# Mixture of experts beside attention: sorting each image's tokens while the next one is attended to

## The chip, the core and the metric

The kernel runs on one core of a Trainium2 chip. The metric is the device time of one execution in microseconds. A core has five engines that each run their own list of instructions in a fixed order and wait for one another through semaphores: TensorE (PE, with its weight loads as PEld), VectorE (DVE), ScalarE (ACT), GpSimd (POOL) and SyncE (SP). Transfers between the device's memory and the core's buffers are issued by SP, ACT or POOL and carried by 16 DMA engines.

## What is computed

Four blocks of a hybrid network work on x of 4 images, 256 channels, 32 x 32 points: 4096 tokens of 256 channels, 1024 to an image. Layer 0 is a Mamba-2 mixer with a squeeze-and-excitation gate, layer 1 a non-local convolution. Layer 3 is an attention of linear kind and an LSTM over 1024 steps. The change is in layer 2:

```python
t = t + _L2_attn_ref(_ln_t(t), Wq, bq, Wk, bk, Wv, bv)      # per image, 1024 x 1024 scores
t = t + _L2_ffn_ref(_ln_t(t), Wg, bg, W1, b1, W2, b2)

# in _L2_ffn_ref, xf = all 4096 tokens, E = 8 experts
gate_logits = xf @ Wg + bg
top_w, top_i = jax.lax.top_k(gate_logits, 2)
top_w = jax.nn.softmax(top_w, axis=-1)
...
h = jax.nn.gelu(xf @ W1[e] + b1[e], approximate=False)
out = out + w_dense[:, e:e + 1] * (h @ W2[e] + b2[e])
```

The normalisation of a token needs only that token, attention needs its image, and which tokens an expert gets needs the gates of all tokens that are counted before.

## The kernel before

x stays in the core's buffers as `s.x`, channels on the partitions, in two halves. The phases run in the order of `PHASES`: `_setup`, `_layer0`, `_layer1`, `_layer2_attention`, `_layer2_experts`, `_layer3` and the LSTM.

`_setup` (L75 to L139) loads x and constants, makes the index tables, and fills `sorted`, a table in the device's memory with 39 x 256 rows of 258 numbers: the normalised token, its weight, and the place where its result goes. Rows that no token takes must be harmless, so 13 transfers of 6 x 128 rows (SP, L137) write zeros and spare places, from two buffers that POOL fills by memset and iota (L132, L133). A pool named `weights` with two buffers holds the weights of a layer (`_weights`, L161).

`_layer2_attention` (L512) multiplies the weights of queries and keys into one matrix `mat` (L528 to L556), normalises all of x over channels (`_layernorm`, L167: PE's averages over the partitions, `mean`, `var`, `wide`), and goes through the images. For an image it makes `q` (L563) and `v` (L576), and then for each of 8 query tiles of 128: scores `p_s` against 1024 keys (L593, 8 matmuls of 512 columns), their maximum (L601 to L603, DVE), exp (L606, ACT), the scale (L610, L611, DVE), 8 transposes (`p_t`, L615), whose copies into `prT` are shared by DVE and ACT (L620, L622). After four query tiles 16 matmuls of 512 columns times the values make the output (L626), which is added to x (L631).

`_layer2_experts` (L763) normalises x again, and `_route` (L634) makes the gates with 64 small matmuls (L649), finds the two best experts of every token, counts by matmul and prefix sum how many tokens each expert has, and gives each expert whole tiles of 256 rows; 2 x 4096 rows fill at most 39 tiles. `_sort` (L737) turns the tokens into rows by transposes and sends 64 scatters of 128 rows (POOL, L757). Then 39 tiles (L784) follow: POOL fetches the weights of the tile's expert (`w`, L786, 128 rows of 16 KB), SP the 256 rows (L793), PE transposes them (`pt`, L801; copy `uT`, L803), 32 matmuls of 256 columns make the hidden layer (`ph`, L808), ACT applies Gelu (L812), 32 more make the output (`po`, L816), DVE scales it (`y`, L821) and POOL scatters it to `results` (L822). Weights, rows and `uT` have three buffers each. A tail (L827 to L852) reads `results` back and adds both shares and the bias to x.

What sets the order: outside of the LSTM, a static scheduler places the instructions of each engine from their dependencies, so an engine's list differs from the order of the code. Pools of buffers are opened and closed; a pool that is opened later may lie on the bytes of a closed one, and its first writer then waits for all users of those bytes.

Of the kernel before, what the change touches and what calls it, by code (L numbers as in the profile page):

```python
# [10 lines left out]
F32 = mybir.dt.float32  # L11
U32 = mybir.dt.uint32
I32 = mybir.dt.int32
# [30 lines left out]
NTILE = 2 * T // TS + E - 1  # L44
ROW = D + 2
# [29 lines left out]
def _setup(s):  # L75
# [50 lines left out]
    s.sorted = nc.dram_tensor("sorted", (NTILE * TS, ROW), F32, kind="Internal").ap()  # L126
    s.results = nc.dram_tensor("results", (2 * T + NTILE * TS, D), F32, kind="Internal").ap()
    n = 6
    with s.tc.tile_pool(name="fill", bufs=2) as pool:
        for i in range(NTILE * TS // P // n):  # L130
            fill = pool.tile([P, n, ROW], F32, name="fill")
            nc.gpsimd.memset(fill[:, :, : D + 1], 0.0)  # L132
            nc.gpsimd.iota(  # L133
                fill[:, :, D + 1 :].rearrange("p a c -> p (a c)"), [[P, n]], base=2 * T + i * n * P,
                channel_multiplier=1, allow_small_or_imprecise_dtypes=True,
            )
            nc.sync.dma_start(  # L137
                s.sorted[bass.ts(i, n * P), :].rearrange("(a p) c -> p a c", p=P), fill
            )  # L139

# [20 lines left out]
def _weights(s, name):  # L161
    w = s.wpool.tile([P, C, NW[name]], F32, name=name, tag="w")
    s.nc.scalar.dma_start(w, s.d[name].rearrange("(k p) n -> p k n", p=P))
    return w
# [37 lines left out]
def _layer0(s):  # L202

    nc, tc = s.nc, s.tc
    w = _weights(s, "w_l0")
    w_zdt, w_xbc = w[:, :, :ZDT], w[:, :, ZDT : ZDT + 512]
    w_out, w_se1 = w[:, :, 772:1028], w[:, :, 1028:1092]
    with ExitStack() as ctx:
# [303 lines left out]
def _layer2_attention(s):  # L512

    nc, tc = s.nc, s.tc
    w = _weights(s, "w_l2")
    s.w_gate = w[:, :, 768:776]
    wq, wk = w[:, :, :D], w[:, :, D : 2 * D]
    scale = D**-0.5
    with ExitStack() as ctx:
        keep = ctx.enter_context(tc.tile_pool(name="l2_keep", bufs=1))  # L520

        mat = keep.tile([P, C, D], F32, name="mat")
        r = keep.tile([P, C], F32, name="r")
        wv = keep.tile([P, C, D + 1], F32, name="wv")
        bv = keep.tile([P, D + 1], F32, name="bv")
        with tc.tile_pool(name="l2_w_ps", bufs=1, space=PSUM) as ps:
            bb = keep.tile([P, C], F32, name="bb")
            nc.vector.tensor_mul(bb, s.col["bq"], s.col["bk"])  # L528
            pm = ps.tile([P, C, D], F32, name="pm")
            pr = ps.tile([P, C], F32, name="pr")  # L530
            pg = ps.tile([P, C], F32, name="pg")
            pb = ps.tile([P, 1], F32, name="pb")
            for m in range(C):
                for k in range(C):
                    nc.tensor.matmul(
                        pm[:, m, :], wq[:, k, bass.ts(m, P)], wk[:, k, :],
                        start=k == 0, stop=k == C - 1,
                    )
                for k in range(C):
                    nc.tensor.matmul(  # L540
                        pr[:, m : m + 1], wk[:, k, bass.ts(m, P)], s.col["bq"][:, k : k + 1],
                        start=k == 0, stop=k == C - 1,
                    )
                for k in range(C):
                    nc.tensor.matmul(
                        pg[:, m : m + 1], wq[:, k, bass.ts(m, P)], s.col["bk"][:, k : k + 1],
                        start=k == 0, stop=k == C - 1,
                    )
            for k in range(C):
                nc.tensor.matmul(pb, s.ones, bb[:, k : k + 1], start=k == 0, stop=k == C - 1)  # L550
            nc.vector.tensor_copy(mat, pm)
            nc.vector.tensor_copy(r, pr)
            nc.vector.tensor_copy(wv[:, :, :D], w[:, :, 2 * D : 3 * D])
            nc.vector.tensor_scalar_mul(wv[:, :, D], pg, scale)
            nc.vector.tensor_copy(bv[:, :D], s.row["bv"])
            nc.vector.tensor_scalar_mul(bv[:, D:], pb, scale)  # L556
# [4 lines left out]
        ps = ctx.enter_context(tc.tile_pool(name="l2_ps", bufs=2, space=PSUM))  # L561
        for b in range(B):
            q = pool.tile([P, C, L], F32, name="q")  # L563
            for m in range(C):
                for i in range(BPI):
                    p = ps.tile([P, W], F32, name="p_mm")
                    for k in range(C):
                        nc.tensor.matmul(
                            p, mat[:, k, bass.ts(m, P)],
                            u[:, k, b * L + i * W : b * L + (i + 1) * W],  # L570
                            start=k == 0, stop=k == C - 1,
                        )
                    nc.scalar.activation(
                        q[:, m, bass.ts(i, W)], p, AF.Identity, bias=r[:, m : m + 1]
                    )
            v = pool.tile([P, TPI, D + 1], F32, name="v")  # L576
            for n in range(TPI):
                p = ps.tile([P, W], F32, name="p_mm")
                for k in range(C):
                    nc.tensor.matmul(  # L580
                        p[:, : D + 1], u[:, k, b * L + n * P : b * L + (n + 1) * P], wv[:, k, :],
                        start=k == 0, stop=k == C - 1,
                    )
                nc.vector.tensor_add(v[:, n, :], p[:, : D + 1], bv)

            for i in range(BPI):
                prT = pool.tile([P, TPI, W], F32, name="prT")
                for j in range(TPB):
# [14 lines left out]
                    nc.vector.tensor_sub(top, c, top)  # L603
                    pr = pool.tile([P, L], F32, name="pr")
# [6 lines left out]
                    nc.vector.tensor_scalar_mul(pr, pr, total)  # L611
                    for g in range(TPI // TPB):
                        p_t = ps.tile([P, TPB, P], F32, name="p_t")
                        for m in range(TPB):
                            nc.tensor.transpose(  # L615
                                p_t[:, m, :], pr[:, bass.ts(g * TPB + m, P)], s.ident
# [6 lines left out]
                for m in range(C):  # L623
                    p = ps.tile([P, W], F32, name="p_mm")
                    for n in range(TPI):
                        nc.tensor.matmul(  # L626
                            p, v[:, n, bass.ts(m, P)], prT[:, n, :],
                            start=n == 0, stop=n == TPI - 1,
                        )
                    xs = s.x[:, m, b, bass.ts(i, W)]  # L630
                    nc.vector.tensor_add(xs, xs, p)  # L631


def _route(s, keep, u):  # L634
# [3 lines left out]
    nc, tc = s.nc, s.tc  # L638
    gate = keep.tile([P, NT, E], F32, name="gate")
    share = keep.tile([P, 2, NT], F32, name="share")  # L640
    slots = keep.tile([P, 2, NT], U32, name="slots")
    wrow = keep.tile([P, NTILE], U32, name="wrow")
    with ExitStack() as ctx:
        pool = ctx.enter_context(tc.tile_pool(name="route", bufs=1))
        ps = ctx.enter_context(tc.tile_pool(name="route_ps", bufs=1, space=PSUM))
        pl = ps.tile([P, NT, E], F32, name="pl")
        for n in range(NT):
            for k in range(C):
                nc.tensor.matmul(  # L649
                    pl[:, n, :], u[:, k, bass.ts(n, P)], s.w_gate[:, k, :],  # L650
                    start=k == 0, stop=k == C - 1,
                )
        lg = pool.tile([P, NT, E], F32, name="lg")
        nc.vector.tensor_add(lg, pl, _bc(s.row["bg"], 1, NT))
        tops, picks = [], []
        for i in range(2):
            top = pool.tile([P, NT], F32, name=f"top{i}")
            nc.vector.tensor_reduce(top, lg, AX.X, ALU.max)
            pick = pool.tile([P, NT, E], F32, name=f"pick{i}")
            nc.vector.tensor_tensor(pick, lg, _bc(top, 2, E), ALU.is_equal)  # L660
            nc.vector.tensor_mul(pick, pick, _bc(s.rank, 1, NT))
            first = pool.tile([P, NT], F32, name=f"first{i}")
            nc.vector.tensor_reduce(first, pick, AX.X, ALU.max)
            nc.vector.tensor_tensor(pick, pick, _bc(first, 2, E), ALU.is_equal)
            if i == 0:
                nc.vector.scalar_tensor_tensor(lg, pick, -3.0e38, lg, ALU.mult, ALU.add)
            tops.append(top)
            picks.append(pick)


        both = pool.tile([P, E, NT], F32, name="both")
        nc.vector.tensor_add(both.rearrange("p e n -> p n e"), picks[0], picks[1])
        flat = both.rearrange("p e n -> p (e n)")
        p_in = ps.tile([P, E, NT], F32, name="p_in")
        nc.tensor.matmul(p_in.rearrange("p e n -> p (e n)"), s.upper, flat, start=True, stop=True)
        p_all = ps.tile([P, E, NT], F32, name="p_all")
        nc.tensor.matmul(p_all.rearrange("p e n -> p (e n)"), s.ones, flat, start=True, stop=True)

        second = share[:, 1, :]
        nc.vector.tensor_sub(second, tops[1], tops[0])  # L680
        nc.scalar.activation(second, second, AF.Exp)
        first = share[:, 0, :]
# [608 lines left out]
```

## Time and profile before

| what | us |
|---|---|
| median of 3 runs (3884.6 to 3886.61) | 3886.4 |
| profiled execution | 3885.56 |
| its span, first to last instruction | 3883.9 |
| layer 0, first `px` (L232) at | 63.2 |
| layer 2's attention, four images | 561.9 to 893.6 |
| second LayerNorm, gates, routing, scatters, first weights | 893.6 to 1081.85 |
| 39 tiles of the experts | 1081.85 to 1676.06 |
| tail, to layer 3's LayerNorm | 1736 |
| LSTM, to the end | 1940 to 3884 |

The profile is taken of one execution. Its page tells for each engine the busy time, cuts the span in 40 slices of 97.1 us with the busy share in tenths, and lists the transfers. A window is a stretch of the span, with each engine's busy time and number of instructions in it, the mean clock granted to TensorE, the share of the DMA engines' time and the GB/s. A line of a group reads: source line, engine, operation, result<-operands, shape, count | busy time and mean ns of one | idle time of the engine just before, and what ended it. PE is busy for 3461.2 of 3883.9 us (89%), DVE 52%, ACT 31%, POOL 9%; the mean granted clock is 0.945.

### The profile page before, as it was taken

The page shows a single profiled execution, that of the slowest core. Times are in us where ns is not written, and L with a number is a line of the kernel's source. Part 1 is how long each engine was busy: PE and PEld are TensorE (multiplying, and loading weights), DVE is VectorE, ACT ScalarE, POOL GpSimd, SP SyncE. Part 2 cuts the span into 40 slices and gives each one's busy share as a digit, 9 for nine tenths or more (in the row PEclk, how much of TensorE's full clock was granted, in tenths as well). Part 3 has the DMA queues.
Part 4 walks back from the last instruction along what each step waited for, and adds up shares of the span by engine and source line. Part 5 has one row for each costly group of instructions (what it writes and reads, how often), then busy time and mean ns, then how long its engine had stood idle before and what let it go on. Part 6 is the DMA issues. An engine that isn't in the chain of part 4 may idle for free.

```text
span 3883.9 us, 147409 instructions
## 1 busy us (share of the span) xinstructions
PE 3461.2 (89%) x65882; PEld 2641.0 (68%) x65882; DVE 2008.8 (52%) x7905; ACT 1220.7 (31%) x4983; POOL 331.4 (9%) x404
## 2 busy tenths in 40 slices
PE   8557769998289999999899999999999999999988
PEld 3344324444178888864588888888888888888776
DVE  3587354342301111113367677777777776777666
ACT  2233212121122222213233343434434334343333
POOL 2055000000611111100000000000000000000000
PEclk8778979997599999998899999999999999999999
DMA  4000000000254554420000000000000000000000
GB/s 173 0 1 1 8 0 0 0 1 0 94 207 167 172 180 165 164 93 0 10 4 5 10 4 5 10 5 10 4 4 10 4 10 4 5 9 5 9 4 9
DMA packets 54619, 152.20 MB, mean 39 GB/s; under 512 B 5464, under 2 KB 42016, under 8 KB 48992
## 3 DMA queue, kind: packets, MB, share of 16 engines
q0 software_dynamic: 12432, 100.64, 7.4%
q1 hardware_dynamic: 39616, 37.39, 3.1%
q8 instruction: 515, 8.44, 0.9%
q10 hardware_dynamic: 1936, 4.75, 0.4%
q14 instruction: 120, 0.98, 0.1%
HBM read 109.58 MB, written 33.18 MB: 37 GB/s over the span
## 4 chain that ended last, share of the span: by engine, by line
PE 71%; DVE 17%; ACT 5%; issue 3%; DMA 2%; POOL 0%; ACTq 0%; DVEq 0%; POOLq 0%; SPq 0%
PE p_c L1142 10%; PE ph L808 7%; PE po L816 7%; DVE turned L1171 6%; PE p_c L1133 6%; PE p_i L1133 4%; PE p_o L1133 4%; PE p_o L1142 4%; PE p_i L1142 4%; PE beside L1086 4%; PE p_mm L626 3%; ACT a_o L1172 2%; DVE hs L1187 2%; DMA sorted<-row,slots 2%; PE p_s L593 2%
## 5 line engine op out<-in xcount | busy, mean ns | idle before, releaser
L1172 ACT ACTIVATE add<-turned 128x8 f32<-128x8 f32 x1024 | 214.4, 209 | 1027.4 <-DVE turned L1171 1027.4
L1142 PE MATMUL p_c<-w_v,hs 128*4 128x64 f32 x16368 | 415.9, 219 | 71.1 <-DVE hs L1187 68.8
L1133 PE MATMUL p_c<-xg,shift 128*128 128x64 f32 x2048 | 445.7, 299 | 0.0
L1142 PE MATMUL p_o<-w_v,hs 128*4 128x64 f32 x16368 | 416.3, 219 | 0.0
L1142 PE MATMUL p_i<-w_v,hs 128*4 128x64 f32 x16368 | 416.0, 219 | 0.0
L1133 PE MATMUL p_i<-xg,shift 128*128 128x64 f32 x2048 | 407.8, 281 | 0.0
L1133 PE MATMUL p_o<-xg,shift 128*128 128x64 f32 x2048 | 396.0, 275 | 0.0
L1171 DVE STREAM_TRANSPOSE turned<-p_c 128x64 f32<-128x64 f32 x1024 | 255.3, 249 | 262.4 <-PE p_c L1142 227.9
L1133 PEld LDWEIGHTS p_c<-xg,shift 128*128 128x128 f32 x2048 | 304.7, 188 | 117.6 <-issue 0.3
L1142 PEld LDWEIGHTS p_c<-w_v,hs 128*4 128x4 f32 x16368 | 227.2, 85 | 193.4 <-DVE hs L1187 120.1
L1133 PEld LDWEIGHTS p_o<-xg,shift 128*128 128x128 f32 x2048 | 310.9, 192 | 0.3
L808 PE MATMUL ph<-uT,w 128*128 128x256 f32 x1248 | 281.2, 384 | 32.6 <-DVE uT L803 28.2
L1133 PEld LDWEIGHTS p_i<-xg,shift 128*128 128x128 f32 x2048 | 304.6, 188 | 0.4 <-issue 0.3
L1187 DVE TENSOR_TENSOR hs<-a_o,th 128x8 f32<-128x8 f32 x1024 | 171.1, 167 | 244.2 <-ACT th L1185 244.2
L812 ACT ACTIVATE hT<-ph,w 128x256 f32<-128x256 f32 x312 | 147.6, 473 | 436.8 <-PE ph L808 436.8
L808 PEld LDWEIGHTS ph<-uT,w 128*128 128x128 f32 x1248 | 235.3, 191 | 72.3 <-DVE uT L803 36.8
L1142 PEld LDWEIGHTS p_o<-w_v,hs 128*4 128x4 f32 x16368 | 281.0, 87 | 0.1
L1142 PEld LDWEIGHTS p_i<-w_v,hs 128*4 128x4 f32 x16368 | 280.9, 87 | 0.1
L816 PE MATMUL po<-w,hT 128*128 128x256 f32 x1248 | 275.7, 379 | 0.0
L1171 DVE STREAM_TRANSPOSE turned<-p_i 128x64 f32<-128x64 f32 x1024 | 272.2, 266 | 0.1
L816 PEld LDWEIGHTS po<-w,hT 128*128 128x128 f32 x1248 | 237.1, 190 | 32.2
L1171 DVE STREAM_TRANSPOSE turned<-p_o 128x64 f32<-128x64 f32 x1024 | 255.4, 249 | 0.2 <-PE p_o L1142 0.2
(312 smaller groups left out, 4572.5 us busy)
## 6 DMA issues: line engine op xcount, KB each, us to landing
sorted<-fill SPq DMA_DIRECT2D x13, 774.0 KB, 4.4
row<-sorted SPq DMA_DIRECT2D x39, 258.0 KB, 2.7
y_in<-results SPq DMA_DIRECT2D x16, 512.0 KB, 4.9
x<-in_x_dram SPq DMA_DIRECT2D x8, 512.0 KB, 9.9
out_dram<-x SPq DMA_DIRECT2D x64, 64.0 KB, 1.7
results<-y,place POOLq DMA_INDIRECT x78, 2.6
w_l<-in_w_l_dram ACTq DMA_DIRECT2D x1, 1092.0 KB
sorted<-row,slots POOLq DMA_INDIRECT x64, 2.5
```

Of the source, the lines that this page charges most:

```text
L593: nc.tensor.matmul(p_s[:, h, :], q[:, k, q0 : q0 + P], u[:, k, b * L + h * W : b * L + (h + 1) * W], start=k == 0, stop=k == C - 1,)
L626: nc.tensor.matmul(p, v[:, n, bass.ts(m, P)], prT[:, n, :], start=n == 0, stop=n == TPI - 1,)
L808: nc.tensor.matmul(ph, w1[:, k, bass.ts(m, P)], uT[:, k, :], start=k == 0, stop=k == C - 1,)
L812: nc.scalar.activation(hT[:, m, :], ph, AF.Gelu, bias=b1[:, m : m + 1])
L816: nc.tensor.matmul(po, hT[:, m, bass.ts(a, P)], w2[:, m, :], start=m == 0, stop=m == NHC - 1,)
L1086: nc.tensor.matmul(p[bass.ts(i, R), :], rows[:, k, bass.ts(g, R)], w_u[:, k, at : at + GQ // GC], start=k == 0, stop=k == C - 1, tile_posi ...
L1133: nc.tensor.matmul(p[:, :H], shift[:, row * B : row * B + P], xg[n][:, g, bass.ts(i, H)], start=True, stop=t == 0,)
L1142: nc.tensor.matmul(p[R * i : R * i + B, :H], hs[:, t - 1, bass.ts(k, B)], w_v[:, k, i * GQ + g * H : i * GQ + (g + 1) * H], start=False, s ...
L1171: nc.vector.transpose(zt.rearrange("p c w -> p (c w)"), pz[g][:, :H])
L1172: nc.scalar.activation(dst.rearrange("p (c b) -> p c b", c=C), zt[:, :, :B], f)
L1187: nc.vector.tensor_mul(h, a_o, th)
```

## The change

`sorted` gets a fixed region of 4096 rows for every expert, and 128 rows behind them for spare rows. It is filled by 32 transfers of 8 x 128 rows from one tile of zeros. With fixed regions a token's row depends only on the tokens ahead of it, so images can be sorted one after another.

`_layer2_weights` now runs second, before layer 0, and leaves `mat`, `wv` and the gates' weights minus their mean in constant buffers. Layers 0, 2 and 3 have weight pools of their own.

`_head` does for one image what LayerNorm, `_route` and `_sort` did for all: it turns x into rows, takes mean and variance by token with bn_stats, rstd by Newton steps on DVE, gates by 8 matmuls in quarters of the array, choice, counts, slots, and 8 row tiles with 16 scatters. It is a generator that yields 89 times; `_layer2_attention` runs parts of the head of image b−1 between the steps of image b's query tiles. `_first_tiles` makes a table of 16 full tiles from the counts of the first three images; these tiles run first, and the last image's head and the table of the other 23 (`_other_tiles`) are parts between their steps. The rows of a tile are fetched by two indirect transfers from POOL. The dependency between the gathers of the 16 full tiles and the last image's scatters, which touch other rows, is left out.

The diff, cut to what the steps need:

```diff
-    s.sorted = nc.dram_tensor("sorted", (NTILE * TS, ROW), F32, kind="Internal").ap()
+    s.sorted = nc.dram_tensor("sorted", (E * T + P, ROW), F32, kind="Internal").ap()
     s.results = nc.dram_tensor("results", (2 * T + NTILE * TS, D), F32, kind="Internal").ap()
-    n = 6
-    with s.tc.tile_pool(name="fill", bufs=2) as pool:
-        for i in range(NTILE * TS // P // n):
-            fill = pool.tile([P, n, ROW], F32, name="fill")
-            nc.gpsimd.memset(fill[:, :, : D + 1], 0.0)
-            nc.gpsimd.iota(
-                fill[:, :, D + 1 :].rearrange("p a c -> p (a c)"), [[P, n]], base=2 * T + i * n * P,
-                channel_multiplier=1, allow_small_or_imprecise_dtypes=True,
-            )
+    n = 8
+    with s.tc.tile_pool(name="fill", bufs=1) as pool:
+        fill = pool.tile([P, n, ROW], F32, name="fill")
+        nc.gpsimd.memset(fill, 0.0)
+        for i in range(E * T // P // n):
             nc.sync.dma_start(
                 s.sorted[bass.ts(i, n * P), :].rearrange("(a p) c -> p a c", p=P), fill
             )
+        last = pool.tile([P, ROW], F32, name="last")
+        nc.vector.memset(last[:, : D + 1], 0.0)
+        nc.vector.tensor_scalar_add(last[:, D + 1 :], s.token[:, :1], float(2 * T))
+        nc.sync.dma_start(s.sorted[E * T :, :], last)
...
-    w = _weights(s, "w_l0")
+    ctx0 = ExitStack()
+    w = _weights(s, ctx0.enter_context(tc.tile_pool(name="l0_w", bufs=1)), "w_l0")
...
+def _layer2_weights(s):
...
+        pool = ctx.enter_context(tc.tile_pool(name="l2_w", bufs=1))
+        ps = ctx.enter_context(tc.tile_pool(name="l2_w_ps", bufs=1, space=PSUM))
+        w = _weights(s, pool, "w_l2")
+        wq, wk, w_gate = w[:, :, :D], w[:, :, D : 2 * D], w[:, :, 768:]
...
+            nc.tensor.matmul(pg, s.avg, w_gate[:, k, :], start=k == 0, stop=k == C - 1)
+        nc.vector.tensor_copy(s.mat, pm)
+        nc.vector.tensor_copy(s.r, pr)
+        nc.vector.tensor_copy(s.wv[:, :, :D], w[:, :, 2 * D : 3 * D])
+        nc.vector.tensor_scalar_mul(s.wv[:, :, D], pc, scale)
+        nc.vector.tensor_copy(s.bv[:, :D], s.row["bv"])
+        nc.vector.tensor_scalar_mul(s.bv[:, D:], pb, scale)
+        nc.vector.memset(s.wg, 0.0)
+        nc.vector.tensor_sub(s.wg[:, :, :E], w_gate, _bc(pg, 1, C))
...
+def _layer2(s):
...
+            one=ctx.enter_context(tc.tile_pool(name="moe_one", bufs=1)),
+            pool=ctx.enter_context(tc.tile_pool(name="moe_head", bufs=2)),
+            w=ctx.enter_context(tc.tile_pool(name="moe_w1", bufs=1)),
+            row=ctx.enter_context(tc.tile_pool(name="moe_row", bufs=3)),
+            scatters=[], full=[],
...
+        first = _layer2_attention(s, m)
+        _layer2_experts(s, m, first)
...
+            parts = _head(s, m, b - 1, psum) if b > 0 else iter(())
+            def beside(n):
+                for _ in range(n):
+                    next(parts, None)
...
                     nc.vector.tensor_sub(top, c, top)
+                    beside(4)
                     pr = pool.tile([P, L], F32, name="pr")
...
                     nc.vector.tensor_scalar_mul(pr, pr, total)
+                    beside(4)
                     for g in range(TPI // TPB):
...
+                    beside(3)
...
+            for _ in parts:
+                pass
+            if b == B - 1:
+                first = _first_tiles(s, m)
+    return first
...
+def _head(s, m, b, psum):
+    nc = s.nc
+    n0 = b * TPI
+    x = m.one.tile([P, TPI, D], F32, name="x_rows")
+    mv = m.pool.tile([P, TPI, 2], F32, name="mv")
+    for n in range(TPI):
+        p = psum()
+        for k in range(C):
+            nc.tensor.transpose(p[:, bass.ts(k, P)], s.xt[:, k, bass.ts(n0 + n, P)], s.ident)
+        yield
+        stats = m.pool.tile([P, nc.vector.BN_STATS_DIM], F32, name="stats")
+        nc.vector.bn_stats(stats, p[:, :D])
+        nc.scalar.copy(x[:, n, :], p[:, :D])
+        yield
+        nc.vector.bn_aggr(mv[:, n, :], stats)
+        yield
...
+    p = psum()
+    for k in range(C):
+        for i in range(Q):
+            nc.tensor.matmul(
+                p[bass.ts(i, R), : L // Q], s.wg[:, k, :],
+                s.xt[:, k, b * L + i * (L // Q) : b * L + (i + 1) * (L // Q)],
+                start=k == 0, stop=k == C - 1, tile_position=(0, R * i),
+            )
+    yield
+    raw = m.pool.tile([P, L // Q], F32, name="raw")
+    nc.scalar.copy(raw, p[:, : L // Q])
...
+    upto = m.pool.tile([P, E, TPI], F32, name="upto")
+    upto_flat = upto.rearrange("p e n -> p (e n)")
+    nc.vector.tensor_tensor_scan(
+        upto_flat, m.go_on.rearrange("p e n -> p (e n)"), p_all, 0.0, ALU.mult, ALU.add
+    )
...
+        nc.vector.tensor_add(m.counts, before, upto[:, :, TPI - 1])
+        nc.vector.tensor_add(at, before, m.first)
...
+    for n in range(TPI):
+        row = m.pool.tile([P, 2, ROW], F32, name="row")
+        nc.vector.tensor_scalar(
+            row[:, 0, :D], x[:, n, :], mv[:, n, :1], rstd[:, n : n + 1], ALU.subtract, ALU.mult
+        )
+        nc.scalar.activation(
+            row[:, 1, :D], x[:, n, :], AF.Identity,
+            bias=shift[:, n : n + 1], scale=rstd[:, n : n + 1],
+        )
+        nc.gpsimd.tensor_copy(row[:, :, D:], pair[:, n])
+        yield
+        for i in range(2):
+            done = nc.gpsimd.indirect_dma_start(
+                m.views[2 * (n0 + n) + i], bass.IndirectOffsetOnAxis(slots[:, i, n : n + 1], 0),
+                row[:, i, :], None,
+            )
+            if b == B - 1:
+                m.scatters.append(done)
+        yield
...
+def _first_tiles(s, m):
...
+    nc.vector.tensor_scalar(edges, m.marks[:, :NCH], float(TS), float(TS), ALU.mult, ALU.add)
+    nc.vector.tensor_tensor(over, _bc(m.counts, 2, NCH), _bc(edges, 1, E), ALU.is_ge)
+    full = m.one.tile([P, E], F32, name="f_full")
+    nc.vector.tensor_reduce(full, over, AX.X, ALU.add)
+    expert, mine, first = _table(s, m, "f", NFULL, full)
...
+    rows = _weight_rows(s, m, "f", expert)
...
+def _other_tiles(s, m, taken):
...
+        wp = body.enter_context(tc.tile_pool(name="moe_w", bufs=2))
+        hp = body.enter_context(tc.tile_pool(name="moe_h", bufs=2))
...
+        def last_image():
+            yield from _head(s, m, B - 1, psum)
+            yield from _other_tiles(s, m, taken)
+        parts = last_image()
+        for j in range(NTILE):
+            if j == NFULL:
+                for _ in parts:
+                    pass
+                rows, slots, added = m.others
+            i = j if j < NFULL else j - NFULL
+            w = (wp if j % 3 else m.w).tile([P, NEXP], F32, name="w")
+            nc.gpsimd.indirect_dma_start(
+                w, None, s.d["w12"], bass.IndirectOffsetOnAxis(rows[:, i : i + 1], 0)
+            )
+            w1 = w[:, : C * HID].rearrange("p (k n) -> p k n", k=C)
+            w2 = w[:, C * HID : C * HID + NHC * D].rearrange("p (k n) -> p k n", k=NHC)
+            b1 = w[:, C * HID + NHC * D :]
+            row = m.row.tile([P, A, ROW], F32, name="row")
+            for a in range(A):
+                got = nc.gpsimd.indirect_dma_start(
+                    row[:, a, :], None, s.sorted,
+                    bass.IndirectOffsetOnAxis(slots[:, i, a : a + 1], 0),
+                )
+                if j < NFULL:
+                    m.full.append(got)
...
+                nc.scalar.activation(hT[:, n, :], ph, AF.Gelu, bias=b1[:, n : n + 1])
+                if n % 2:
+                    next(parts, None)
+                    next(parts, None)
...
+        for got in m.full:
+            for put in m.scatters:
+                for one, other in ((got, put), (put, got)):
+                    tc.declare_no_dep(
+                        one.ins, other.ins, reason="the last image's rows follow those of full tiles"
+                    )
...
+        s.wpool = ctx.enter_context(s.tc.tile_pool(name="l3_w", bufs=1))
...
-    w = _weights(s, "w_l3")
+    w = _weights(s, s.wpool, "w_l3")
...
-    _setup, _layer0, _layer1, _layer2_attention, _layer2_experts, _layer3,
+    _setup, _layer2_weights, _layer0, _layer1, _layer2, _layer3,
...
-    s.wpool = ctx.enter_context(tc.tile_pool(name="weights", bufs=2))
```

## The prediction

> **What bounds the kernel now.** I read the slices of the page first, to see where PE stops, then windows over these stretches, the chain of waits across them, the fill tile, and one image of attention by line. The whole kernel is a chain through PE, with two holes:
>
> ```profile
> PE   8557769998289999999899999999999999999988
> ...
> PEclk8778979997599999998899999999999999999999
> DMA  4000000000254554420000000000000000000000
> ```
>
> A slice is 97.1 us. In slices 9 to 11 PE falls and its clock goes to half: that is the LayerNorm, gates and sorting between attention and experts. In slice 0 the DMA engines work: loads and the fill of `sorted`. The windows (PE busy first, the last three columns are clock, DMA share, GB/s) and the chain give the sizes:
>
> ```profile
> 26.00:30.00 4.00, 4.00 (x10) 1.46 (x9) 1.22 (x1) 0.33 (x1) 1.97 (x3) 1.00 1.00 341
> 26.00:56.00 30.00, 23.39 (x38) 6.50 (x37) 13.12 (x10) 5.13 (x5) 14.04 (x20) 0.75 0.79 269
> ...
> 893.60:943.00 49.40, 42.72 (x81) 12.32 (x80) 23.31 (x18) 10.42 (x10) 0.18 (x1) 0.85 0.00 0
> 943.30:971.00 27.70, 27.48 (x128) 27.38 (x128) 0.49 (x4) 0.00 (x0) 0.00 (x0) 0.50 0.00 1
> 971.00:983.00 12.00, 2.05 (x4) 1.18 (x4) 10.11 (x31) 1.51 (x2) 0.00 (x0) 0.50 0.21 66
> 983.00:1067.00 84.00, 20.30 (x64) 9.66 (x64) 22.15 (x136) 11.93 (x32) 60.67 (x63) 0.50 0.28 98
> ```
> ```profile
> 1067.05 2.49 DMA sorted<-row,slots
> 1071.46 10.35 DMA w<-in_w_dram,wrow
> 1081.85 8.83 PE ph L808 x32
> ```
>
> Attention's last matmul ends at 893.6. Then come 49.4 us of LayerNorm, 27.5 of gates, 12 of DVE routing, 84 of scatters (POOL sends 64, one per 1.3 us) and 15 until the first expert weights are there: 188.2 us to the first `ph` at 1081.85. This is what the change attacks. The fill costs nothing today: layer 0 starts beside it, and only one thing waits for its end:
>
> ```profile
> who waited for it (us, times):
>   POOL fill L132: 32.7, 11
>   POOL xbc L213: 4.7, 1
> ```
>
> That second line is the warning. `xbc` has no data from the fill; it waits because its pool lies on bytes that the fill pool gave back.
>
> **Basis.** The profiled execution took 3885.56 us (span 3883.9, 1.66 around it), 0.84 under the median of 3886.4.
>
> **1. The start: +119.** The new `sorted` has 32,896 rows of 1032 bytes, 33.95 MB instead of 10.3. Layer 2's weight pool is now opened second and lies on the closed fill pool. In the instruction order of the changed kernel, ACT's load of `w_l2` waits for the last fill on all the fill's semaphores. PE's order opens with the matmuls on these weights, so the first LayerNorm's `mean`, which stands behind them, waits too, and `w_l0` lies on `w_l2`'s bytes. So nothing of layer 0 starts before the fill ends. Its rate is not on view with 32 transfers in a row. The windows with the DMA engines full (share 1.00) show 341 GB/s, those from 20 to 23 us 332; I take 336. With only two tiles in turn it was 269 at a share of 0.79. The weights and images around 14 to 20 us reached 397. So: loads before the fill end at 14.4 (3.2 + 4.5 MB at about 400); 33.95 MB at 336 is 101 us, 115.7; its end 1.3 later, 117; `w_l2` 4.4 (as the 768 KB load of `w_l3`) 121.4; the weight product 3.6 warm in before (477.13 to 480.7), about 6 at half clock with its copies 6.4: 127.8. LayerNorm as layer 1's, 49.8: 177.6; up to `px` 4.3: 181.9. In before `px` L232 began at 63.2. Difference +119. By 397 GB/s the fill is 85 us, +102; by 269 it is 127, +145.
>
> The Trainium skill, page "DMA: Bandwidth & Descriptors", section "Specifications", gives about 358 GB/s as one core's limit towards HBM. An estimate by that page is 95 us of fill and some 6 us less in the sum; the window with 397 GB/s here is above that figure.
>
> **2. The weight product leaves layer 2: −1.** The copies stood at 508.96 to 510.5, right after layer 1; matmuls were hidden there already.
>
> **3. Images 1 to 3 with a head beside them: +33.** An image takes 82.1 us now, with PE at 77.5 (8 x 3.44 `p_s`, 8 x 1.05 transposes, 6.87 `q`, 7.1 `v`, 27.5 `av`). The rows of one image:
>
> ```profile
> L593 PE MATMUL p_s<-u,q 128*128 128x512 f32 x64 | 28.9, 594 | 0.9 <-ACT pr L606 0.9
> ...
> L601 DVE TENSOR_REDUCE top<-p_s 128x1 f32<-128x1024 f32 x8 | 9.8, 1224 | 7.4 <-PE p_s L593 7.4
> ...
> L615 PE MATMUL p_t<-ident,pr 128*128 128x128 f32 x64 | 8.8, 282 | 3.6 <-DVE pr L611 3.6
> ...
> L611 DVE TENSOR_SCALAR pr<-pr,total 128x1024 f32<-128x1024 f32 x8 | 6.0, 751 | 0.2
> ```
>
> From `p_s` to the transposes the chain is 1.22 + 0.21 + 0.16 on DVE, 1.11 + 0.19 exp, 0.16 + 0.75 on DVE = 3.8 us; the next `p_s` covers 3.44. So PE already waits about half a microsecond per query tile, and what DVE puts into that chain comes on top. A head brings PE 16 transposes (2.1), 8 gate matmuls of 256 columns (at `po`'s 6.92 / 32 = 0.216 each, 1.7), 2 transposes and 2 counts (0.6): 4.4. It brings DVE some 17 us: 8 bn_stats and 8 row writes at 0.42 (as the sort's copies of 256 elements, L749), about 55 small ones at 0.16 to 0.21 (as L602 and L603); DVE has 31 of 82 busy, so it has room. It brings POOL 16 scatters of 0.96. Floor per image 4.4, with all else in gaps. Upper end 18: of the 8 parts put between the steps of each query tile's chain, seven at 0.25 stand in it, 1.7 x 8 = 13.6, plus 4.4. What decides for the middle is the row ring: two row buffers, each free only when its scatters have landed (0.96 + 2.5), and ACT's and DVE's row writes wait for that with the next `prT` copies queued behind them. Following the order by hand I get 3.6 in an image's first half and about 8 in its second (some 5 of it that wait): 12, 12 and 9. Range 13 to 55.
>
> **4. From attention to the first `ph`: −176.6.** Where 188.2 us stood there are now the last scatters of image 2, a small table on DVE, and tile 0's gathers. POOL has tile 0's weight load ahead of the last scatters, and what POOL sends after a weight load lands with it: results scatter after `w` at 1126.0 landed at 1137.2. Then six gathers of 1 us, 2.5 landing, transposes and the copy `uT`: 11.6 us. Bounds 4 (nothing queued) and 15: −184 to −173.
>
> **5. The tiles: +15.8.** 39 tiles at 15.30 (7.17 `ph`, 6.92 `po`, 1.2 gap) now have the last image's head within tiles 0 to 4: PE 4.4; `uT` of tile 4 behind row writes that wait for scatters, about 7; about 1 in tile 3; a first tile at a cold clock +2; against the 594.2 measured +1.4 from rounding to the steady period. ACT changes between Exp and Gelu (1.28 a table load), covered by three `ph` buffers; without them +2.6. Range 8 to 25. The later tiles keep their period: gathers take 78 x 0.96 = 75 us more of POOL, which has 109 of 594 busy, and `row` is asked for three tiles ahead.
>
> **6. Tail, layer 3, LSTM: 0.** Their weights now load after the tail, 4.4 us, beside LayerNorm's 50.
>
> **Sum:** 119 − 1 + 33 − 176.6 + 15.8 = −9.8, so 3875.8 on the profiled execution's basis, about 3876. What a measurement can tell from no change is 0.2%, 7.8 us. So the gain of the sort is nearly eaten by the larger fill.
>
> **Rivals.**
> - *The fill is faster, or the heads fit into gaps* (+102, or +15 for the heads): 3859 or 3858, both 3841; about 3855. For it: 397 GB/s exists in the trace. Against: that was with rows of 3 to 4 KB, and PE's waits.
> - *The fill does not hold the start* (its pool's bytes not waited for, so the change does not do what I read): 3757. Only `xbc`'s wait and the order speak, both against it.
> - *Slower: the fill at the rate of two in flight,* 269 GB/s. 127 us, place: the first 145 us, 3902. It decides from 286 GB/s downwards (118.6 us); at 306 the two kernels are equal. For it: the long window of 30 us. Against: that one had to wait for POOL's memsets, the new one does not. A fill paced like the single transfers (774 KB in 4.4 us, 176 GB/s) would take 193 us: 3968.
> - *Slower: DVE or the row ring becomes the bound of a query tile,* 20 a head rather than 11: 3903.
> - *Slower: the period of the tiles grows,* because `row` comes from POOL behind `w`: 1 us each, 3915. The Trainium skill, same page, section "Issuing engine by pattern", speaks against this move: simple loads belong to Sync, whose path is called generally faster. It has no price there; the rows show 2.7 us for SP's `row` and 2.5 for POOL's scatters.
>
> **How the numbers follow.** Forecast (3866 to 3886): 0.38, of it 0.20 faster and 0.18 same. Fast fill or cheap heads 0.22; fill not waited for 0.03; slow fill 0.14; DVE or ring 0.13; period 0.07; far above 0.03. From the slower cases 0.04 end within 0.2%. Faster 0.45, same 0.22, slower 0.33. Range 3844 to 3910: outside lie the fill not waited for, the lower end of cheap (0.06), most of period (0.05), far above and the tops of the slow ones (0.03), 0.20 together.
>
> **What would show it.** The last `sorted<-fill` landing near 117 and `px` near 182; images 1 to 3 at 91 to 94 us with waits of ACT's rows on scatters; about 12 us between the last `p_mm` and the first `ph`; tiles at 15.3 after the fourth or fifth. I am wrong if PE is busy in layer 0 before the fill has landed, if the images stay at 86 or pass 100, or if tiles 20 to 38 take 16.

## The result and the profile after

The changed kernel takes 3894.8 us (median of 12 runs, 3892.0 to 3900.8) against 3885.6 for the kernel before (12 runs): ratio 1.0024, with a 95% interval of 1.0015 to 1.0033. The forecast was 9.8 us less; it became 9.2 more. The profiled execution has a span of 3893.4 us, 9.5 above that of before. Stage by stage, from the two traces:

| stage | before | after | difference | forecast |
|---|---|---|---|---|
| to attention's first matmul | 561.9 | 699.35 | +137.4 | +118 |
| four images | 331.7 | 364.4 | +32.7 | +33 |
| attention's end to first `ph` | 188.2 | 12.1 | −176.2 | −176.6 |
| 39 tiles | 594.2 | 610.1 | +15.9 | +15.8 |
| tail, layer 3, LSTM | 2207.8 | 2207.5 | −0.3 | 0 |
| sum | | | +9.5 | −9.8 |

Four rows of five are as forecast; the first one alone turns the sign. The slices of the changed kernel's page show both sides of the trade:

```profile
PE   0592866989889999999899999999999999999988
...
PEclk9995988899999999998999999999999999999999
DMA  9400000000155444530000000000000000000000
```

The hole that was in slices 9 to 11 is gone, and a new one stands in slice 0 and the first third of slice 1, where PE does nothing while the DMA engines fill `sorted`. The windows of the changed kernel (PE busy first; the last columns are clock, DMA share and GB/s) are: the fill, image 0 without a head, image 1 with one, the gap, the tiles.

```profile
40.00:100.00 60.00, 0.00 (x0) 0.00 (x0) 0.00 (x0) 0.00 (x0) 0.00 (x0) 1.00 1.09 295
...
699.35:784.05 84.70, 80.19 (x240) 41.38 (x241) 30.02 (x59) 18.15 (x29) 0.00 (x0) 0.96 0.00 0
784.05:878.30 94.25, 84.20 (x279) 43.85 (x278) 43.00 (x135) 24.11 (x46) 17.31 (x24) 0.93 0.07 23
1063.70:1075.80 12.10, 2.24 (x10) 1.56 (x9) 1.90 (x6) 0.00 (x0) 7.67 (x8) 0.68 0.38 98
1075.80:1685.90 610.10, 574.16 (x2682) 495.56 (x2682) 87.50 (x253) 159.19 (x333) 197.76 (x209) 0.99 0.47 167
```

In the first of them no engine works at all: 295 GB/s, with the DMA engines full. The answer on the tile `last`, whose transfer is the fill's end, names who stood behind it:

```profile
who waited for it (us, times):
  POOL xbc L219: 128.4, 1
  DVE bb L537: 123.6, 1
```

`bb` is the first operation of `_layer2_weights`, a product of two columns of constants that is written to the new weight pool (PE's first matmul follows it at 132.6), and `xbc` belongs to layer 0. Neither reads a byte of the fill. The chain of waits at the jump from attention to the experts:

```profile
1048.95 8.31 DMA sorted<-row,slots
...
1061.29 0.98 POOL sorted L872
...
1062.58 2.93 DMA sorted<-row,slots
...
1065.77 0.99 POOL row L1052
...
1072.11 2.73 DMA row<-sorted,f_slots
...
1075.03 0.70 DVE uT L1069
...
1075.78 5.49 PE ph L1074 x12
```

The last scatters of image 2, a landing, row gathers of about 1 us each, a landing, the copy, and the first `ph`: the sequence that was forecast, 12.1 us for 11.6. The first line is a scatter that POOL sent behind tile 0's weight load (at 1045.49): it landed after 8.31 us, where the median of all 64 scatters is 2.8.

### The profile page after: what moved, and what is told of

The parts are those of the page before. It is cut to its first block, busy times and chain, and to the rows that moved or that the text cites. A ratio compares the mean times of both kernels' runs of the same rounds, so it can differ in the third digit from the quotient of the medians.

```text
span 3893.4 us, 147430 instructions
## 1 busy us (share of the span) xinstructions
PE 3397.3 (87%) x65762; PEld 2606.6 (67%) x65762; DVE 2016.6 (52%) x8082; ACT 1228.0 (32%) x5013; POOL 399.5 (10%) x490
## 4 chain that ended last, share of the span: by engine, by line
PE 70%; DVE 16%; ACT 5%; SPq 3%; issue 3%; DMA 2%; POOL 1%; ACTq 0%; DVEq 0%; POOLq 0%
PE p_c L1417 10%; PE ph L1074 7%; PE po L1085 7%; DVE turned L1446 7%; PE p_c L1408 6%; PE p_i L1408 4%; PE p_o L1408 4%; PE p_o L1417 4%; PE p_i L1417 4%; PE beside L1361 4%; SPq L138 3%; PE p_mm L695 3%; PE p_s L659 2%; ACT a_o L1447 2%; DVE hs L1462 2%
```

## The experiments

A run is compared with runs beside it, since the same kernel differs by some us from group to group: the kernel before took 3893.8 us (7 runs) beside the first four runs (long rows, bytes kept, large fill, three in flight) and 3883.6 us (15 runs) beside the others, on another chip. The changed kernel was run again only beside the others, so the first four are read by the moments in their traces as well. A time with no number of runs is that of one execution, without an interval.

### Long rows in the fill

```diff
-                s.sorted[bass.ts(i, n * P), :].rearrange("(a p) c -> p a c", p=P), fill
+                s.sorted[bass.ts(i, n * P), :].rearrange("(p a) c -> p a c", p=P), fill
```

> The changed kernel, with one edit: each of the 32 fills writes, from a partition, 8 rows that lie side by side (8256 bytes in one piece) instead of 8 rows that lie 128 rows apart (1032 bytes each). Same bytes, same zeros. Theory A (the fill is paced by its small pieces): the fill goes from 295 GB/s to about the 420 GB/s that loads with long rows show in the changed kernel's windows at 8 to 14 us, so from about 115 us to 81, and all that stands behind it comes earlier: the last fill lands near 98 instead of 132 and the time is about 3861. Theory B (writes to the device's memory are the limit, whatever their pieces): 295 GB/s again, about 3895.

Measured: 3862.5 us, 31.3 below the kernel before beside it, and in the window of the fill:

```profile
20.00:80.00 60.00, 0.00 (x0) 0.00 (x0) 0.00 (x0) 0.00 (x0) 0.00 (x0) 1.00 1.01 422
```

The fill's last transfer landed at 96.4 instead of 132.1, and the first `px` moved by the same, from 202.0 to 166.3. Theory A: the same bytes, from the same tile, to the same rows, are paced by the length of the pieces.

### The fill's bytes kept

```diff
-    n = 8
-    with s.tc.tile_pool(name="fill", bufs=1) as pool:
+    n = 4
+    for pool in (s.const,):
```

> The changed kernel, with the tile of zeros and the tile of spare rows taken from the constant pool (and 64 fills of 4 rows a partition, as there is room for no more), so that no later pool lies on their bytes. Theory A (the start is held only because layer 2's and layer 0's weight pools, and xbc, lie on the bytes of the closed fill pool): the fill runs beside layer 0, the first px comes near 75 instead of 202, and the time is about 3768. Theory B (the weight loads stand behind the fill on the DMA engines, or layer 0 suffers from a fill beside it): px not before 120, time above 3810.

Measured: 3774.0 us (4 runs), 0.969 of the kernel before (0.9674 to 0.9706). The rows of the first `px` matmuls, in the changed kernel and in this run, and this run's window of the fill:

```profile
L238 PE MATMUL px<-u,w_l x128: 592/592/1219, 202.0 to 284.3; 128*128 128x512 f32 x128
...
L238 PEld LDWEIGHTS px<-u,w_l x128: 190/190/338, 77.1 to 158.5; 128*128 128x128 f32 x128
...
20.00:140.00 120.00, 109.09 (x264) 48.77 (x265) 39.35 (x52) 28.02 (x45) 0.00 (x0) 0.89 1.07 261
```

The first `px` came at 77.1. The fill ran from 13 to about 155, at 261 GB/s between 20 and 140 (294 in the changed kernel, with fills of twice the size and nothing beside them), and layer 0 did not suffer from it: from `px` to attention's first matmul are 496.4 us here and 497.4 in the changed kernel. Theory A: the 125 us by which `px` moved are the price of a pool's address, not of the fill.

### The large fill in the kernel before

```diff
+        extra = nc.dram_tensor("extra", (22 * 8 * P, ROW), F32, kind="Internal").ap()
+        more = pool.tile([P, 8, ROW], F32, name="more", bufs=1)
+        nc.gpsimd.memset(more, 0.0)
+        for i in range(22):
+            nc.sync.dma_start(
+                extra[bass.ts(i, 8 * P), :].rearrange("(a p) c -> p a c", p=P), more
+            )
```

> The kernel before, with 22 more transfers of 8 x 128 rows of zeros to a table of their own after its 13 fills, from a tile of the same fill pool: 33.6 MB written in all, nothing else changed. Theory A (the wait is for the bytes of the fill pool): xbc waits for the last of them, about 56 + 23.3 MB at 295 GB/s = 135 us, layer 0's first px or its copy comes some 75 us later than in the kernel before, time about 3960. Theory B (a larger fill alone, beside layer 0, costs nothing): 3886.

Measured: 3963.9 us, 70.1 above the kernel before. The answer on the tile `more`'s table:

```profile
who waited for it (us, times):
  DVE xbc L245: 77.3, 1
  POOL xbc L220: 66.8, 1
```

Theory A. The line that was harmless before (`xbc`, 4.7 us) is the whole price as soon as the fill is long. Here layer 0's LayerNorm still ran beside the fill, its weights lying elsewhere, so the price is 70 and not 125.

### Three fills in flight, and two

```diff
+        fills = [pool.tile([P, n, ROW], F32, name=f"fill{k}") for k in range(3)]
+        for fill in fills:
+            nc.gpsimd.memset(fill, 0.0)
         for i in range(E * T // P // n):
+            fill = fills[i % 3]
+            if i > 2:
+                nc.gpsimd.memset(fill[:, :1, :1], 0.0)
```

> The changed kernel, with three tiles of zeros in turn and a memset of one column ahead of each reuse, so that no more than three fills are in flight, where the changed kernel has about four (each lands 15.2 us after it was issued, one every 3.5 us). Theory A (the rate falls with the number in flight; in the kernel before, the bursts with two in flight showed 345 to 350 GB/s): about 330 GB/s, 103 us, time about 3882. Theory B (the sustained rate is what it is): 295 GB/s or less, 3895 or more.

Measured: 3903.1 us, 9.2 above the kernel before beside it, as the changed kernel was in the first measurement, and 286 GB/s from 20 to 120. Theory B. The same with two tiles:

> As the run with three in flight, with two tiles of zeros in turn: two fills in flight, as in the kernel before, but with a memset of one column between them instead of 1.5 us of POOL. Theory A (two in flight of these short rows run at 340 to 350 GB/s, three or more at 290): windows at 340 GB/s while both run, some gaps, on the whole about 310 GB/s, fill 110 us, about 5 us less than the changed kernel. Theory B (the bursts of the kernel before were fast because each followed a pause, and the sustained rate is 290): windows at 290 and gaps on top, on the whole 270 GB/s or less, 126 us, some 10 us more than the changed kernel.

Measured: 3901.6 us, 4.7 above the changed kernel's median beside it. The window of the fill:

```profile
20.00:120.00 100.00, 0.00 (x0) 0.00 (x0) 0.00 (x0) 0.00 (x0) 2.55 (x26) 1.00 1.02 285
```

Neither theory has the number: 285, where A said about 310 and B 270 or less. The 4.7 us are not the fill's: `px` began at 204.2 here and at 204.3 in the changed kernel beside it, attention even 1.4 us earlier, and the whole difference between the two profiles lies behind the experts' tiles. Cut into pieces of a quarter of a microsecond, the stretch from 45 to 55 us goes between 78 and 376 GB/s. So bursts of 340 to 355 do exist with these rows, and slack follows. The number in flight isn't what sets the mean: with two, three and four it is 285, 286 and 294. Why the bursts end is not settled.

### Pairs of rows

```diff
-                s.sorted[bass.ts(i, n * P), :].rearrange("(a p) c -> p a c", p=P), fill
+                s.sorted[bass.ts(i, n * P), :].rearrange("(b p a) c -> p b a c", p=P, a=2),
+                fill.rearrange("p (b a) c -> p b a c", a=2)
```

> The changed kernel, with two rows side by side in each piece of a fill (2064 bytes instead of 1032; 8256 gave 422 GB/s, 4128 gave 406 beside layer 0). Theory A (each piece costs a fixed time on its DMA engine beside its bytes: from 1032 bytes at 295 and 8256 at 422 GB/s, with 16 engines, 56.0 and 313 ns a piece, so 35.6 ns a kilobyte and 19 fixed): 2064 bytes take 93 ns, 356 GB/s, a fill of 95 us, about 20 us less than the changed kernel. Theory B (short of some length the rate is that of the short rows): 295 GB/s, no change. Theory C (over 2 kB the rate is full): 415 GB/s, 33 us less.

Measured: 3867.9 us, 29.0 below the changed kernel beside it, and steady:

```profile
20.00:80.00 60.00, 0.00 (x0) 0.00 (x0) 0.00 (x0) 0.00 (x0) 0.00 (x0) 1.00 1.06 379
```

Between A (356) and C (415); theory B fell. By 16 engines, a piece of 1032, 2064 and 8256 bytes took 56, 87 and 313 ns (16 x bytes / rate). A line through the two longer ones has about 12 ns a piece beside the bytes; the 1032-byte piece lies 7 ns above it. So a fixed time a piece, which is an estimate from these rates, explains most, not all, of the slow fill.

### The changed kernel again

> The changed kernel unedited, so that the runs beside it can be compared with it on the same chip. It should stand to the kernel before as measured, 1.0024.

Measured: 3896.9 us (6 runs), ratio 1.0032 (1.0019 to 1.0044): the small loss stands in a second set of runs.

### Eight row buffers for a head

```diff
-        row = m.pool.tile([P, 2, ROW], F32, name="row")
+        row = m.pool.tile([P, 2, ROW], F32, name="row", bufs=8)
```

> The changed kernel with eight buffers instead of two for the row tiles of a head, one for each of its 8 row tiles; nothing else. Theory A (half of what a head costs is ACT's and DVE's row writes waiting for scatters, with the attention's own copies and maxima queued behind them): the three images with a head lose about 5 us each, the wait ahead of the ph of the fifth tile goes (8.35 us in the changed kernel), time about 22 less than the changed kernel's. Theory B (a head costs what its instructions take on PE and DVE, wherever they wait): within 5 us of the changed kernel.

Measured: 3874.5 us (10 runs), 22.4 below the changed kernel beside it, ratio to the kernel before 0.9976 (0.9966 to 0.9985). The waits of the changed kernel between 784 and 1064 us (who <- for whom: total, times, longest) show what went; the three lines on `sorted` are absent in this run's answer, and PE's is 12.6:

```profile
ACT row L865 <- DMA sorted<-row,slots: 38.0, 17, 8.9
...
DVE row L862 <- DMA sorted<-row,slots: 34.4, 16, 8.0
...
PE p_t L683 <- DVE pr L678: 27.8, 5, 9.2
...
POOL row L869 <- DMA sorted<-row,slots: 5.5, 2, 4.9
```

Against the changed kernel beside it, the images with a head became shorter by 6.5, 4.3 and 3.4 us, and the jump from attention to the first `ph` by 6.4, from 12.2 to 5.8. Theory A has the sum; one part of it fell. The wait in the tiles did not go, the tiles became shorter by 1.4 us only. It moved from the fifth tile to the sixth, and the timeline (start, duration, engine, line; in brackets the idle time before) names the cause:

```profile
1129.37 0.98 POOL L1044 DMA_INDIRECT w<-in_w_dram,f_rows  x1 [0.30 <-DMA sorted<-row,slots]
...
1131.94 0.98 POOL L1052 DMA_INDIRECT row<-sorted,f_slots  x1 [0.31 <-issue]
1133.23 0.97 POOL L1052 DMA_INDIRECT row<-sorted,f_slots  x1 [0.30 <-issue]
...
1139.44 0.17 DVE L1061 CAST place<-row 128x2 uint32<-128x2 f32 x1 [19.86 <-DMA row<-sorted,f_slots]
...
1141.04 2.50 PE L1074 MATMUL ph<-uT,w 128*128 128x256 f32 x5 [6.88 <-DVE uT L1069]
```

POOL sent the head's scatters first, then the weights of a later tile, then this tile's rows, which landed behind the weights: 6.1 us after the second was sent, 2.73 in the chain above. In the changed kernel it is the fifth tile that waits: its `uT` stands behind a row write on DVE (at 1148.4) that waited for a scatter.

### All of it together

```diff
-    with s.tc.tile_pool(name="fill", bufs=1) as pool:
+    s.fill = ExitStack()
+    for pool in (s.fill.enter_context(s.tc.tile_pool(name="fill", bufs=1)),):
...
+    s.fill.close()
     nc, tc = s.nc, s.tc
     with ExitStack() as ctx:
         m = SimpleNamespace(
...
-    _setup, _layer2_weights, _layer0, _layer1, _layer2, _layer3,
+    _setup, _layer0, _layer2_weights, _layer1, _layer2, _layer3,
```

with long rows (here 4 side by side, 4128 bytes a piece, in 64 fills) and the eight row buffers as above.

> Three edits together: the fill pool stays open until layer 2 (64 fills of 4 rows a partition), the fills write rows that lie side by side, layer 2's weight product stands behind layer 0, and eight row buffers for a head. If the start was held by the bytes alone: px near 63 as in the kernel before, so 139 less than the changed kernel, and 22 less from the ring: 161 less than the changed kernel, about 3735 by the first measurement. If the ring is nothing: about 3757. If the fill beside layer 0 costs DMA time that layer 0 needs: more than 3770.

Measured: 3737.1 us (4 runs), ratio to the kernel before 0.9625 (0.9609 to 0.9641), 159.8 below the changed kernel. `px` begins at 61.8, attention at 560.0 (561.9 before), and the fill runs beside layer 0 at

```profile
20.00:80.00 60.00, 49.36 (x99) 18.05 (x99) 26.66 (x23) 11.82 (x15) 0.00 (x0) 0.80 1.03 405
```

with 49 of 60 us of PE busy in the same window, where the changed kernel had none.

## Why the prediction was wrong

**Step 1, the start: the step that failed.** The mechanism was right: nothing of layer 0 before the fill's end, with `bb`, PE's weight product, `mean` and `w_l0` in a row behind it. The size was not: +118 forecast at attention's start (119 less 1), +137.4 measured. Of these 19.4 us:

- 15.1 are the fill, a term that was mis-sized. The step put it so: "The windows with the DMA engines full (share 1.00) show 341 GB/s, those from 20 to 23 us 332; I take 336." The last fill landed at 132.1 and not at 117. The rate over 100 us was 294 GB/s; the same bytes in pieces of 2064 and 8256 bytes went at 379 and 422, so the length of the piece set it. The windows of 3 and 4 us were bursts of a transfer that paused every few us. The 30 us window at 269 was put aside because its fills waited for POOL's memsets; with that wait cut to a memset of 0.1 us, and nothing beside them, two in flight made 285, so the pauses had cost at most 16 GB/s and not the way to 336. (14.4 and 101 are also 115.4 and not the 115.7 that was written.)
- 2.0 are the weight load and product: `mean` began 12.8 after the fill's end, 10.8 forecast. The load took its 4.4. The forecast had priced a slow product: "about 6 at half clock" for 3.6 before. It came out at 7.0; `pm` took 634 ns a matmul in the changed kernel's row (below) and 379 in the row of before, while the granted clock of the window reads 1.00, so the profile doesn't say what slowed it. Another 1 us is four matmuls for the mean of the gates' weights (L556, 143.6 to 144.6), which the kernel before does not have and the forecast left out.

```profile
L550 PE MATMUL pm<-w_l x8: 634/634/792, 136.8 to 141.6; 128*128 128x256 f32 x8
```

- 3.0 are the LayerNorm up to `px`: 57.1 for 54.1. It is not a slower start: the first `mean` matmuls follow each other every 0.85 us here, and so they do in the LayerNorm of before that the estimate came from, whose window begins at a granted clock of 0.50. The time went at the end of the averages. The new order leaves only four `var` matmuls for the end, behind a wait of 2.46 us for ACT, and they took 3.15 us at a granted clock of 0.58, where before eight took 3.60 behind a wait of 0.74 (changed kernel first):

```profile
176.70 3.15 PE L189 MATMUL var<-sq,avg_row 128*8 128x512 f32 x4 [2.46 <-ACT sq L187]
...
538.76 3.60 PE L184 MATMUL var<-sq,avg_row 128*8 128x512 f32 x8 [0.74 <-ACT sq L182]
```

- The other −0.7 is step 2 and rounding.

The rival on the slower side (the fill at the rate of two in flight) came nearest. It put the line at 306 GB/s for equal times and 286 for slower by 0.2%. With 294 GB/s alone the sum gives 3890, short of the 3893.3 that are 0.2% above the kernel before; the 5 us of the product and the LayerNorm carried it past that. The rival's reason did not hold: two, three or four fills in flight ran at nearly the same rate.

**Step 2** held: attention starts 137.4 later where `px` starts 138.8 later, −1.4 for −1.

**Step 3** held in size (12.1, 10.7 and 10.3 us for images 1 to 3, forecast 12, 12 and 9) and in cause: the row ring's waits are shown by the eight buffers, 14.2 us of the 32.7. DVE did not become the bound: with the ring widened, image 1 takes 87.9 us, 5.8 over the 82.1 of before, of which PE's own additions were put at 4.4 (in the changed kernel's windows PE's busy time is 4.0 longer with a head than without).

**Step 4** held in size, and the queue behind the weights is there: the scatter at 1048.95 landed after 8.31 us. It counted because the next row write had to wait for it. With eight buffers POOL sent all of image 2's scatters ahead of the weights and the jump took 5.8 us; that run takes the ring's wait and the queue away together, so it doesn't tell their shares.

**Step 5** held in size and in place: from the first tile's `ph` to the sixth's are 91.1 us for 75.2 before, which is all of the 15.9, and the other 34 tiles take 519.0 us in both. The wait ahead of the fifth tile's `ph` was 8.35, where about 7 was forecast. But its cause is double: remove the ring, and POOL's order of scatters, weights and gathers is late next at 6.9. With the later tiles unchanged, the rival on the moved gathers fell.

**The other rivals:** a fill that isn't waited for fell with `bb`'s wait of 123.6 us, and became true in the run with the fill's bytes kept: 119.8 us below the kernel before beside it, where 3757 would have been 129 below. There `px` came at 77.1, 14 later than before, as the weight product stands ahead of the first LayerNorm (61.8 with the product behind layer 0). The fill paced like the single transfers, 3968, was far off; 774 KB of 1024 bytes in 4.4 us are also 180 GB/s and not 176.

## What to carry to other kernels

A transfer that nobody reads for a long time still holds up whoever is given its buffer's bytes: when a fill grows, look for the pools that will lie on them, and keep its buffer open until the transfer is surely over. Take the rate of a long transfer from a window as long as it, of the same piece length, and not from the best few microseconds; where the pieces are short, lay them side by side. And where two large terms nearly cancel, the sign hangs on the larger one's error: 336 against 294 GB/s was enough.

## What the runs showed of the hardware that was not expected

- Writes from the core's buffers to the device's memory ran at 294 GB/s with pieces of 1032 bytes, 379 with 2064, 405 with 4128 (beside layer 0) and 422 with 8256, the DMA engines being full in all four. Beside layer 0, pieces of 1032 bytes ran at 261 (64 fills of half the size).
- The Trainium skill, page "DMA: Bandwidth & Descriptors", section "Specifications", names 512 bytes as the least for line rate, and its section "Why small descriptors are slow (HBM only)" gives about 3 cycles of fixed cost a packet. An estimate from that second figure, 33 beats and 3 more for 1032 bytes, is a loss of 8%. The runs lost 30% from 8256 to 1032 bytes, so for these writes the measurement decides.
- With pieces of 1032 bytes, windows of 100 us had a DMA share of 1.09 with three and four transfers in flight and 1.02 with two; the higher share brought hardly more bytes (286 and 294 GB/s for 285).
- A fill at 405 GB/s beside layer 0 cost that layer nothing that the trace shows: `px` at 61.8 and attention at 560.0, 63.2 and 561.9 before.
